# Causal attention with experts on one core: score products cut from four passes to two and three, operands split into a leading and a trailing part

## The chip, the cores and the metric

The kernel runs on one core of a Trainium2 chip. The metric is the device time of one execution in microseconds (us). Three executions of the kernel before took 3232.03, 3232.71 and 3240.1 us; the median is 3232.71 us.

## The reference

The input is x of 32 sequences, 512 tokens and 256 channels, in float32. Sixteen heads of 16 channels attend causally, twice:

```
q, k = x @ W_attn + b_attn          # queries and keys
y    = softmax(mask(q k^T / 4)) x   # first attention: the values are x itself
e    = x[1:] - y[:-1]               # what the first attention missed
k2   = x[:-1] @ W_k2 + b_k2
y2   = softmax(mask(q[1:] k2^T / 4)) e   # second attention, same queries
x    = layernorm(x + proj(y) + proj(y2))
x    = layernorm(x + experts(x))    # experts' output on one block of 512 tokens, in the first sequence
```

The softmax is taken with its true row maximum subtracted, so every score is needed twice: once for the maximum, once for the exponential. The results are float32.

## The kernel before

**Tiling.** A "group" is four heads of one sequence: 4 groups per sequence, 128 in all. The four heads of a group lie in the four quadrants of 32 partitions (rows) of SBUF; a head has 16 channels, so 16 rows of a quadrant are spare. The tiles `q_t` (5 buffers) and `kk_t` (6 buffers, with the keys of both attentions as index a = 0 and a = 1) hold one group each. A matmul between two quadrants uses 32 rows of TensorE, so four heads can stream side by side.

**Steps and slots.** `step(n)` runs for each group number n. It has five slots. In a slot, `slot(n, u)` issues on TensorE, interleaved by hand, two kinds of products: `maxima` for group n (scores with queries down the partitions, so VectorE can reduce the row maximum, L240) and `scores` for groups n-2 and n-3 (scores with keys down the partitions, of which ScalarE takes the exponential, L290, and GpSimd zeroes what lies above the diagonal, L294). In each slot each head has 512 columns of either kind. The heads are handled as two pairs; a slot takes four of PSUM's buffers `ps`, which are all four that there are. Between the slots other TensorE work stands in the lists `rest[0]` to `rest[4]`: `project` (L170), `augment` (transposes of the maxima, L248), `values` (products of the probabilities and the values, L335), `normalize` (transposes back, L350), `turn` and `attended` (output projection, L404 and L416). TensorE's order is exactly this one; the other engines' orders are set by a scheduler.

**The maximum.** It is written into a spare row of the quadrant through `augment`, added to the queries by GpSimd into `qm` (L253), and the keys carry a -1 in that row (from `b_qkk2`, put in by L133 and L136). One product then yields score minus maximum.

**The projection and its copies.** `project(two, m)` makes the queries (m = 0), the keys (m = 1) or the second keys (m = 2) of two groups at once, 2 x `two` and 2 x `two` + 1, with the heads packed densely. ScalarE adds the bias into `pk` (L174). One DMA for each head, on SP's queue, then carries 16 rows of 2 KB into the head's quadrant (L185): 8 DMAs for each m. In step n, `two` is n // 2 + 1. Before, m = 0 is projected in slot 1 of an even step, m = 1 and m = 2 in slots 1 and 2 of the odd step after it; the first group of the two is used from slot 0 of the next even step on.

**Experts.** Steps 10 to 17 also run one expert each (`hidden`, `down`, `load_expert`).

All products of `maxima` and `scores` are float32. The trace has two matmul records for each of them (L221: 12288 records, L275: 8192).

Of the kernel before, what the change touches and what calls it, by code (L numbers as in the profile page):

```python
# [9 lines left out]
F32 = mybir.dt.float32  # L10
BF16 = mybir.dt.bfloat16
# [11 lines left out]
NEG = -3.0e38  # L23
ALPHA = 1.702
LIMIT = 7.0


@with_exitstack
def block_kernel(
# [45 lines left out]
    bq_sb = const.tile([P, 3, NG], F32, name="bq_sb")  # L75
    nc.sync.dma_start(bq_sb, b_qkk2)
# [9 lines left out]
    q_t = [const.tile([P, T], F32, name=f"q_t{i}") for i in range(5)]  # L86
# [3 lines left out]
    bp_sb = const.tile([P, C], F32, name="bp_sb")  # L90
    nc.scalar.dma_start(bp_sb, b_proj.broadcast_to([P, C]))
    bp2 = const.tile([P, C], F32, name="bp2")
    nc.vector.tensor_add(bp2, bp_sb, bp_sb)
# [29 lines left out]
    v_pad = const.tile([P, NB, NG * GH, HS], F32, name="v_pad")  # L123
    e_pad = const.tile([P, NB, NG * GH, HS], F32, name="e_pad")
# [6 lines left out]
    zero = mx[0].rearrange("p n h s -> p (n h s)")  # L131
    for t in q_t:
        nc.scalar.activation(t, zero, AF.Identity, bias=bq_sb[:, 0, 0:1])  # L133
    for t in kk_t:
        for m in range(2):
            nc.scalar.activation(t[:, m], zero, AF.Identity, bias=bq_sb[:, 1 + m, 0:1])  # L136
# [5 lines left out]
    def load(b):  # L142
        s = seqs[b] = {}
        s["xT"] = seq.tile([P, NC, T], F32, tag="xT", name=f"xT{b}")
        nc.sync.dma_start(s["xT"], xT[b].rearrange("(c p) t -> p c t", p=P))
        s["x"] = seq.tile([P, NB, C], F32, tag="x", name=f"x{b}")
        nc.sync.dma_start(s["x"], x[b].rearrange("(n p) c -> p n c", p=P))
# [9 lines left out]
    def prepare(n):  # L157
        b, g = divmod(n, NG)
        s = seqs[b]
        heads = slice(g * GH, (g + 1) * GH)  # L160
        nc.gpsimd.tensor_copy(
            v_pad[:, :, heads, 0:HD], s["x"].rearrange("p n (h d) -> p n h d", d=HD)[:, :, heads]
        )


    def project(two, m):
        b, half = divmod(two, NG // 2)
        ps = bank2(f"pj{two}_{m}")
        for c in range(NC):
            nc.tensor.matmul(  # L170
                ps[:, 0], wq_sb[:, m, c, half * P : (half + 1) * P], seqs[b]["xT"][:, c], start=(c == 0), stop=(c == NC - 1)
            )
        pk = work.tile([P, T], F32, tag=f"half{(two * 3 + m) % 2}", name=f"pk{two}_{m}", bufs=1)
        nc.scalar.activation(pk, ps[:, 0], AF.Identity, bias=bp_qk[:, m, half : half + 1])  # L174
        for k in range(2):
            n = 2 * two + k
            d = groups.setdefault(n, {})
            if m == 0:
                t = d["q"] = q_t[n % len(q_t)]
            else:  # L180
                d["kk"] = kk_t[n % len(kk_t)]
                t = d["kk"][:, m - 1]
            for h in range(GH):
                r = (GH * k + h) * HD
                nc.sync.dma_start(t[HS * h : HS * h + HD], pk[r : r + HD])  # L185
# [12 lines left out]
    def maxima(n, u, pair):  # L198

        d = groups[n]  # L200
        parts, first, step, kinds = units[u]
        ps = bank2(f"sm{n}_{u}_{pair}")
        blocks = ps.rearrange("p h (k c) -> p h k c", c=P)
        work = []


        def mask(c, hh, rows):
            nc.tensor.matmul(  # L208
                blocks[:, hh, first::step, HS * c :],
                pick[rows, c],  # L210
                hide[rows, c, kinds[0] : kinds[1], HS * c :],
                start=(c == 0),
                stop=False,
            )

        for c in (0, *range(NB - 1, 0, -1)):
            work.append(((kinds[1] - kinds[0]) * (P - HS * c), partial(mask, c)))
        views = []

        def score(view, i, a, na, keys, stop, hh, rows):  # L220
            nc.tensor.matmul(  # L221
                view[:, hh, :, keys],
                d["q"][rows, i * P : (i + 1) * P],
                d["kk"][rows, a : a + na, keys],
                start=False,
                stop=stop,
            )

        for i, a, na, at in parts:
            nk = (i + 1) * P  # L230
            view = ps[:, :, at * P : at * P + na * nk].rearrange("p h (a k) -> p h a k", k=nk)
            views.append((view, mx[n % 2][:, i, NH2 * pair : NH2 * (pair + 1), HD + a : HD + a + na]))
            order = [slice(i * P, nk), slice(0, i * P)] if i else [slice(0, P)]
            for keys in order:
                stop = at == parts[-1][3] and keys == order[-1]
                work.append((4 * na * (keys.stop - keys.start), partial(score, view, i, a, na, keys, stop)))

        def largest():
            for view, to in views:
                nc.vector.tensor_reduce(to, view, AX.X, ALU.max)  # L240

        return work, largest

    def augment(n):
        d = groups[n]
        ps = bank2(f"mt{n}")
        for i in range(NB):
            nc.tensor.transpose(  # L248
                ps[:, 0, i * P : (i + 1) * P], mx[n % 2][:, i].rearrange("p h s -> p (h s)"), ident
            )  # L250
        d["qm"] = grp.tile([P, T], F32, tag="qm", name=f"qm{n}")
        nc.scalar.copy(d["qm"], ps[:, 0])  # L252
        nc.gpsimd.tensor_add(d["qm"], d["qm"], d["q"])  # L253
# [12 lines left out]
    def scores(n, u, pair):  # L266
        parts = [p for p in banks[u] if 0 <= n - p[0] < n_all]
        if not parts:
            return [], lambda: None
        ps = bank2(f"sc{n}_{u}_{pair}")  # L270
        pt = work.tile([P, NH2, T], F32, tag=f"pt{u}", name=f"pt{n}_{u}_{pair}")
        todo = []

        def score(d, a, j, at, hh, rows):
            nc.tensor.matmul(  # L275
                ps[:, hh, at * P : at * P + T - j * P],
                d["kk"][rows, a, j * P : (j + 1) * P],
                d["qm"][rows, j * P :],
                start=True,
                stop=True,  # L280
            )

        for a, j, at in parts:
            groups[n - a]["pt", a, j, pair] = pt[:, :, at * P : at * P + T - j * P]
            todo.append((4 * (T - j * P), partial(score, groups[n - a], a, j, at)))

        def exponentials():
            lo = parts[0][2] * P
            hi = parts[-1][2] * P + T - parts[-1][1] * P
            nc.scalar.activation(pt[:, :, lo:hi], ps[:, :, lo:hi], AF.Exp, scale=HD**-0.5)  # L290

            for a, j, at in parts:
                diag = pt[:, :, at * P : (at + 1) * P]
                nc.gpsimd.affine_select(  # L294
                    diag, diag, pattern=[[0, NH2], [1, P]], compare_op=ALU.is_ge, fill=0.0, base=-a,
                    channel_multiplier=-1,
                )

        return todo, exponentials
# [27 lines left out]
    def values(n, a):  # L327
# [5 lines left out]
        for j in order:  # L333
            for h in range(GH):
                nc.tensor.matmul(  # L335
                    ps[HS * h : HS * (h + 1), 0, j * P :],
                    vals[:, j, g * GH + h, :],
# [7 lines left out]
    def normalize(n, a):  # L345
# [20 lines left out]
        if a == 0:  # L366
# [3 lines left out]
            nc.gpsimd.tensor_sub(e_pad[:, :, g * GH : (g + 1) * GH, 0:HD], heads(s["xs"]), heads(s["y"]))  # L370
        else:
            y2 = work.tile([P, NB, GH * HD], F32, tag="y2", name=f"y2_{n}")
# [21 lines left out]
    def turn(b):  # L394
        s = seqs[b]

        s["xr"] = seq.tile([P, NB, C], F32, tag="xr", name=f"xr{b}", bufs=1)
        nc.sync.dma_start(s["xr"], x[b].rearrange("(n p) c -> p n c", p=P))
        nc.gpsimd.tensor_add(s["xr"], s["xr"], bp2.unsqueeze(1).to_broadcast([P, NB, C]))
# [7 lines left out]
    def attended(b, half):  # L407
# [6 lines left out]
        for i in range(2):  # L414
# [9 lines left out]
            s["h"][:, two], ps[:, 0].rearrange("p (i c) -> p i c", c=C), s["xr"][:, two]  # L424
# [59 lines left out]
    def load_expert(e):  # L484
        gu = moe["gu", e] = seq.tile([P, NC, 2, NF * P], F32, tag="gu", name=f"gu{e}")
# [3 lines left out]
        bd = moe["b_dn", e] = seq.tile([1, C], F32, tag="bd", name=f"bd{e}")  # L489
        nc.sync.dma_start(bd, b_dn[:, e])  # L490

    def hidden(e, f):
# [13 lines left out]
        for k in range(2):  # L506
            t = work.tile([P, T], F32, tag=f"half{k}", name=f"hf{e}_{f}_{k}", bufs=1)
            nc.vector.tensor_scalar(t, ps[:, k], moe["b_gu"][:, e, k, f : f + 1], LIMIT, ALU.add, ALU.min)  # L508
            half.append(t)
# [32 lines left out]
    def step(n):  # L542
# [3 lines left out]
        if r == 1 and b + 1 < B:  # L546
# [5 lines left out]
        if ready(n - 1):  # L552
            rest[3].append(lambda: augment(n - 1))
        if ready(n - 3):
            rest[1].append(lambda: normalize(n - 3, 0))
            rest[3].append(lambda: values(n - 3, 1))
            rest[4].append(lambda: normalize(n - 3, 1))
        two = n // 2 + 1
        if ready(2 * two):
            for m, s in [(0, 1)] if n % 2 == 0 else [(1, 1), (2, 2)]:  # L560
# [7 lines left out]
        if r2 == NG - 1 and 0 <= b2 < B:  # L568
            rest[0].append(lambda: attended(b2, 0))
            rest[2].append(lambda: attended(b2, 1))  # L570
# [98 lines left out]
```

## Time and profile before

| what | value |
|---|---|
| profiled execution: time, span | 3235.08 us, 3233.4 us |
| median of three executions | 3232.71 us |
| mean granted TensorE clock | 0.987 |
| PE (TensorE matmul) busy | 3057.4 us, 95% |
| PEld (weight load) busy | 1947.3 us, 60% |
| DVE (VectorE) busy | 1867.3 us, 58% |
| ACT (ScalarE) busy | 1734.0 us, 54% |
| POOL (GpSimd) busy | 1538.0 us, 48% |
| DMA | 148.12 MB, SP's queue 16.0% of the 16 DMA engines |

Busy time is the union of an engine's records. Matmuls on different quadrants overlap, so sums of matmul durations are larger than the time that they take. L12 is line 12 of the program text; `SPq` is SP's sequencer, which issues DMAs and is not counted as busy.

### The profile page before, as it was taken

The page shows a single profiled execution, that of the slowest core. Times are in us where ns is not written, and L with a number is a line of the kernel's source. Part 1 is how long each engine was busy: PE and PEld are TensorE (multiplying, and loading weights), DVE is VectorE, ACT ScalarE, POOL GpSimd, SP SyncE. Part 2 cuts the span into 40 slices and gives each one's busy share as a digit, 9 for nine tenths or more (in the row PEclk, how much of TensorE's full clock was granted, in tenths as well). Part 3 has the DMA queues.
Part 4 walks back from the last instruction along what each step waited for, and adds up shares of the span by engine and source line. Part 5 has one row for each costly group of instructions (what it writes and reads, how often), then busy time and mean ns, then how long its engine had stood idle before and what let it go on. Part 6 is the DMA issues. An engine that isn't in the chain of part 4 may idle for free.

```text
span 3233.4 us, 97999 instructions
## 1 busy us (share of the span) xinstructions
PE 3057.4 (95%) x42312; PEld 1947.3 (60%) x42312; DVE 1867.3 (58%) x2864; ACT 1734.0 (54%) x1956; POOL 1538.0 (48%) x2975
## 2 busy tenths in 40 slices
PE   5998889899999999999999999999999999999997
PEld 3665545566666666666666666666666666666664
DVE  4664444566666656566665666666556666665662
ACT  2554444455555555555555555555555555555554
POOL 4443434354554445454544455454445555544555
PEclk9999989999999999999999999999999999999998
DMA  4111111111111111111111111111111111111100
GB/s 113 32 32 49 41 39 37 39 52 46 46 41 54 38 54 48 53 45 38 50 41 51 51 50 51 41 41 54 38 54 48 53 45 44 45 47 44 39 26 21
DMA packets 144240, 148.12 MB, mean 46 GB/s; under 512 B 40984, under 2 KB 108992, under 8 KB 143808
## 3 DMA queue, kind: packets, MB, share of 16 engines
q1 hardware_dynamic: 143296, 141.42, 16.0%
q8 instruction: 333, 5.46, 0.7%
q14 instruction: 99, 0.81, 0.1%
q10 hardware_dynamic: 416, 0.39, 0.0%
q0 software_dynamic: 96, 0.04, 0.0%
HBM read 74.63 MB, written 16.78 MB: 28 GB/s over the span
## 4 chain that ended last, share of the span: by engine, by line
PE 61%; ACT 7%; POOL 7%; DVE 4%; issue 3%; SPq 0%; ACTq 0%; POOLq 0%; DMA 0%; DVEq 0%
PE sm L221 13%; PE av L335 13%; PE sc L275 12%; PE pj L170 10%; ACT pt L290 7%; PE po L416 4%; PE yt L350 3%; PE sm L208 3%; POOL h L445 2%; POOL pt L294 2%; PE mt L248 2%; DVE st L438 1%; DVE h L423 1%; POOL qm L253 1%; DVE mx L240 1%
## 5 line engine op out<-in xcount | busy, mean ns | idle before, releaser
L240 DVE TENSOR_REDUCE mx<-sm 128x2 f32<-128x1024 f32 (+3 forms) x1792 | 1541.1, 914 | 1092.1 <-PE sm L221 1083.0
L290 ACT ACTIVATE pt<-sc 128x1024 f32<-128x1024 f32 (+1 forms) x1282 | 1295.6, 1023 | 551.7 <-PE sc L275 529.4
L275 PE MATMUL sc<-qm,kk_t 32*128 32x256 f32 (+3 forms) x8192 | 1384.3, 448 | 26.2 <-ACT pt L290 7.8
L294 POOL TENSOR_SCALAR_AFFINE_SELECT pt<-pt 128x256 f32<-128x256 f32 x2048 | 797.3, 409 | 1268.5 <-ACT pt L290 1249.3
L221 PE MATMUL sm<-kk_t,q_t 32*128 32x128 f32 (+2 forms) x12288 | 1286.0, 351 | 12.8 <-DMA kk_t<-pk 12.8
L221 PEld LDWEIGHTS sm<-kk_t,q_t 32*128 32x128 f32 x12288 | 909.7, 187 | 29.3 <-DMA kk_t<-pk 13.6
L275 PEld LDWEIGHTS sc<-qm,kk_t 32*128 32x128 f32 x8192 | 711.1, 185 | 349.3 <-issue 206.9
L208 PE MATMUL sm<-hide,pick 32*128 32x128 bf16 (+5 forms) x10240 | 541.1, 216 | 8.5 <-DVE mx L240 7.8
L343 ACT COPY avs<-av 128x512 f32<-128x512 f32 x256 | 150.0, 586 | 533.8 <-PE av L335 533.8
L170 PE MATMUL pj<-xT,wq_sb 128*128 128x512 f32 x768 | 386.2, 627 | 29.5 <-DMA xT<-in_xT 19.5
L208 PEld LDWEIGHTS <-pick 32*128 32x128 bf16 x10240 | 351.4, 92 | 84.2 <-issue 67.4
L335 PE MATMUL av<-pt,v_pad 128*32 128x512 f32 (+3 forms) x4096 | 309.5, 437 | 41.6 <-POOL pt L294 40.7
L335 PE MATMUL av<-pt,e_pad 128*32 128x512 f32 (+3 forms) x4096 | 309.8, 443 | 10.8 <-DVE hf L508 3.6
L174 ACT ACTIVATE pk<-pj,bp_qk 128x512 f32<-128x512 f32 x192 | 131.9, 687 | 316.0 <-PE pj L170 219.6
L335 PEld LDWEIGHTS av<-pt,v_pad 128*32 128x32 f32 x4096 | 116.8, 109 | 223.1 <-issue 136.6
L170 PEld LDWEIGHTS pj<-xT,wq_sb 128*128 128x128 f32 x768 | 133.9, 194 | 167.9 <-issue 97.3
L335 PEld LDWEIGHTS av<-pt,e_pad 128*32 128x32 f32 x4096 | 124.3, 111 | 160.8 <-issue 126.3
L350 PE MATMUL yt<-ident,avs 128*128 128x128 f32 x1024 | 169.8, 289 | 21.1 <-ACT pt L290 20.3
L253 POOL TENSOR_TENSOR qm<-qm,q_t 128x512 f32<-128x512 f32 x128 | 163.9, 1281 | 16.9 <-ACT qm L252 9.6
L445 POOL TENSOR_SCALAR h<-h,mv,r 128x256 f32<-128x256 f32 x124 | 151.0, 1224 | 6.5
L350 PEld LDWEIGHTS yt<-ident,avs 128*128 128x128 f32 x1024 | 108.5, 142 | 65.9 <-ACT pt L290 50.5
L416 PE MATMUL po<-wp_sb,ysT 128*128 128x256 f32 x512 | 129.0, 396 | 5.3 <-ACT ysT L405 1.1
(78 smaller groups left out, 1442.8 us busy)
## 6 DMA issues: line engine op xcount, KB each, us to landing
kk_t<-pk SPq DMA_DIRECT2D x1024, 32.0 KB
xT<-in_xT SPq DMA_DIRECT2D x32, 512.0 KB
x<-in_x SPq DMA_DIRECT2D x32, 512.0 KB
q_t<-pk SPq DMA_DIRECT2D x512, 32.0 KB
xr<-in_x SPq DMA_DIRECT2D x32, 512.0 KB
out<-h SPq DMA_DIRECT2D x31, 512.0 KB
xs<-in_x SPq DMA_DIRECT2D x32, 384.0 KB
gu<-in_w_gu SPq DMA_DIRECT2D x8, 512.0 KB
```

Of the source, the lines that this page charges most:

```text
L170: nc.tensor.matmul(ps[:, 0], wq_sb[:, m, c, half * P : (half + 1) * P], seqs[b]["xT"][:, c], start=(c == 0), stop=(c == NC - 1))
L208: nc.tensor.matmul(blocks[:, hh, first::step, HS * c :], pick[rows, c], hide[rows, c, kinds[0] : kinds[1], HS * c :], start=(c == 0), stop ...
L221: nc.tensor.matmul(view[:, hh, :, keys], d["q"][rows, i * P : (i + 1) * P], d["kk"][rows, a : a + na, keys], start=False, stop=stop,)
L240: nc.vector.tensor_reduce(to, view, AX.X, ALU.max)
L253: nc.gpsimd.tensor_add(d["qm"], d["qm"], d["q"])
L275: nc.tensor.matmul(ps[:, hh, at * P : at * P + T - j * P], d["kk"][rows, a, j * P : (j + 1) * P], d["qm"][rows, j * P :], start=True, stop ...
L290: nc.scalar.activation(pt[:, :, lo:hi], ps[:, :, lo:hi], AF.Exp, scale=HD**-0.5)
L294: nc.gpsimd.affine_select(diag, diag, pattern=[[0, NH2], [1, P]], compare_op=ALU.is_ge, fill=0.0, base=-a, channel_multiplier=-1,)
L335: nc.tensor.matmul(ps[HS * h : HS * (h + 1), 0, j * P :], vals[:, j, g * GH + h, :], d["pt", a, j, h // NH2][:, h % NH2], start=(j == orde ...
L350: nc.tensor.transpose(ps[:, 0, i * P : (i + 1) * P], d["avs", a][:, i * P : (i + 1) * P], ident)
L416: nc.tensor.matmul(ps[:, 0, i * C : (i + 1) * C], s["ysT"][:, c, (2 * half + i) * P : (2 * half + i + 1) * P], wp_sb[:, c], start=(c == 0) ...
L445: nc.gpsimd.tensor_scalar(t[:, i], t[:, i], mv[:, k, 0:1], r[:, k : k + 1], ALU.subtract, ALU.mult)
```

## The change

The products become float32r products (a bit view of the same tiles, `half`), for which the operands are first split: `lead` is the projection written as float32r by ScalarE, `tail` is what is left of it, written by VectorE from the same PSUM bank.

- A key's quadrant holds the lead in its first 16 rows and the tail in its last 16 rows. The queries get two planes: plane 0 has the lead in both halves of the quadrant, plane 1 the tail in both. Plane 0 with the keys gives lead x (lead + tail), plane 1 gives tail x (lead + tail).
- `maxima` issues two such products where it had one float32 product, and the masks no longer open the bank.
- `scores` issues three: two with the planes and a third one, of the constants `minus` with the transposed maxima `m`, which subtracts the maximum. `qm` and its addition go; in their place two small GpSimd operations split the maxima.
- The copies into the quadrants are 32 DMAs for m = 0 (four per head) and 16 for m = 1 and for m = 2 (two per head).
- Work moves: m = 2 is projected in slot 2 of the even step, m = 1 in slot 1 and m = 0 in slot 2 of the odd step; `augment` and both `normalize` go to slot 0, both halves of `attended` to slot 1. The separate load of x for the output (`xr`) goes, `x` has 3 buffers, `v_pad` and `e_pad` are packed at 17 columns per head, experts' `gu` and `bd` have one buffer.

```diff
-        pk = work.tile([P, T], F32, tag=f"half{(two * 3 + m) % 2}", name=f"pk{two}_{m}", bufs=1)
-        nc.scalar.activation(pk, ps[:, 0], AF.Identity, bias=bp_qk[:, m, half : half + 1])
+        bias = bp_qk[:, m, half_ : half_ + 1]
+        lead = work.tile([P, T], F32, tag="half0", name=f"lead{two}_{m}")
+        nc.scalar.activation(half(lead), ps[:, 0], AF.Identity, bias=bias)
+        tail = work.tile([P, T], F32, tag="half1", name=f"tail{two}_{m}")
+        nc.vector.scalar_tensor_tensor(half(tail), ps[:, 0], bias, lead, ALU.add, ALU.subtract)
...
-                nc.sync.dma_start(t[HS * h : HS * h + HD], pk[r : r + HD])
+                first, second = slice(HS * h, HS * h + HD), slice(HS * h + HD, HS * (h + 1))
+                if m == 0:
+                    for rows in (first, second):
+                        nc.sync.dma_start(d["q"][rows, 0], lead[r : r + HD])
+                        nc.sync.dma_start(d["q"][rows, 1], tail[r : r + HD])
+                else:
+                    nc.sync.dma_start(d["kk"][first, m - 1], lead[r : r + HD])
+                    nc.sync.dma_start(d["kk"][second, m - 1], tail[r : r + HD])
...
         def score(view, i, a, na, k, start, stop, hh, rows):
             nc.tensor.matmul(
-                view[:, hh, :, keys],
-                d["q"][rows, i * P : (i + 1) * P],
-                d["kk"][rows, a : a + na, keys],
-                start=False,
+                view[:, hh],
+                half(d["q"][rows, k, i * P : (i + 1) * P]),
+                half(d["kk"][rows, a : a + na, : (i + 1) * P]),
+                start=start,
                 stop=stop,
             )
...
+        nc.gpsimd.tensor_copy(half(t[:, :, :, 0:2]), top)
+        nc.gpsimd.tensor_sub(half(t[:, :, :, 2:4]), top, t[:, :, :, 0:2])
...
-        nc.scalar.copy(d["qm"], ps[:, 0])
-        nc.gpsimd.tensor_add(d["qm"], d["qm"], d["q"])
+        nc.scalar.copy(half(d["m"]), ps[:, 0])
...
-        def score(d, a, j, at, hh, rows):
+        def score(d, a, j, at, k, hh, rows):
+            keys = minus[a][rows] if k == 2 else d["kk"][rows, a, j * P : (j + 1) * P]
+            queries = d["m"][rows] if k == 2 else d["q"][rows, k]
...
-            todo.append((4 * (T - j * P), partial(score, groups[n - a], a, j, at)))
+            for k in range(3):
+                todo.append((T - j * P, partial(score, groups[n - a], a, j, at, k)))
...
         if ready(n - 1):
-            rest[3].append(lambda: augment(n - 1))
+            rest[0].append(lambda: augment(n - 1))
         if ready(n - 3):
-            rest[1].append(lambda: normalize(n - 3, 0))
+            rest[0].append(lambda: normalize(n - 3, 0))
             rest[3].append(lambda: values(n - 3, 1))
-            rest[4].append(lambda: normalize(n - 3, 1))
+        if ready(n - 4):
+            rest[0].append(lambda: normalize(n - 4, 1))
         two = n // 2 + 1
         if ready(2 * two):
-            for m, s in [(0, 1)] if n % 2 == 0 else [(1, 1), (2, 2)]:
+            for m, s in [(2, 2)] if n % 2 == 0 else [(1, 1), (0, 2)]:
                 rest[s].append(lambda m=m: project(two, m))
...
-            rest[0].append(lambda: attended(b2, 0))
-            rest[2].append(lambda: attended(b2, 1))
+            for h in range(2):
+                rest[1].append(lambda h=h: attended(b2, h))
```

## The prediction

> **What bounds the kernel now.** First the page: busy time, the chain that ended last, the costliest groups, the DMA issues.
>
> ```profile
> PE 3057.4 (95%) x42312; PEld 1947.3 (60%) x42312; DVE 1867.3 (58%) x2864; ACT 1734.0 (54%) x1956; POOL 1538.0 (48%) x2975
> ...
> PE 61%; ACT 7%; POOL 7%; DVE 4%; issue 3%; SPq 0%; ACTq 0%; POOLq 0%; DMA 0%; DVEq 0%
> ...
> L275 PE MATMUL sc<-qm,kk_t 32*128 32x256 f32 (+3 forms) x8192 | 1384.3, 448 | 26.2 <-ACT pt L290 7.8
> ...
> L221 PE MATMUL sm<-kk_t,q_t 32*128 32x128 f32 (+2 forms) x12288 | 1286.0, 351 | 12.8 <-DMA kk_t<-pk 12.8
> ...
> kk_t<-pk SPq DMA_DIRECT2D x1024, 32.0 KB
> ```
>
> TensorE never rests, and the chain runs through it. SP and DMA have 0% of the chain: the copies into the quadrants (1024 for keys, 512 for queries, L185) are free now. Is TensorE saturated in the steady part too? The table by stretches for four steps (columns: length, busy us of PE, PEld, DVE, ACT, POOL, clock, DMA share, GB/s):
>
> ```profile
> 1535.00:1628.00 93.00, 90.53 (x1312) 58.56 (x1310) 56.40 (x87) 52.05 (x60) 45.84 (x89) 1.00 0.17 47
> ```
>
> Yes: 90.5 of 93 us at full clock, the others under 61%. The L248 transposes of groups 40 and 120 start at 1162.15 and 3024.83 us in the timeline, so a pair of steps (even, odd) takes 1862.68 / 40 = **46.57 us**. The timeline of TensorE prices one slot and its neighbours:
>
> ```profile
> 1583.74 0.49 PE L275 MATMUL sc<-qm,kk_t 32*128 32x384 f32 x2
> ...
> 1584.07 0.48 PE L275 MATMUL sc<-qm,kk_t 32*128 32x384 f32 x2
> ...
> 1584.39 0.27 PE L275 MATMUL sc<-qm,kk_t 32*128 32x128 f32 x2
> ...
> 1584.87 0.66 PE L350 MATMUL yt<-ident,avs 128*128 128x128 f32 x4
> ```
>
> A float32 product is two records; the 384-column records start 0.325 us apart, two passes each: 0.42 ns per column and pass. In the same timeline this slot runs from 1582.53 to 1584.87 (2.34 us). The five slots of that step sum to 12.3, mean 2.46; transposes take 0.6, a projection 1.89, values 2.29, both output halves 3.84, `turn` 0.97 (mean distances to the next start).
>
> Then SP's timeline, the timeline of the kernel's start (the one place where TensorE waits for a copy), and the table by stretches for the same start:
>
> ```profile
> 1573.02 11.14 SPq L185 DMA_DIRECT2D kk_t<-pk  x16
> ```
>
> ```profile
> 38.76 9.48 SPq L185 DMA_DIRECT2D kk_t<-pk  x14
> ...
> 40.70 4.00 PE L221 MATMUL sm<-kk_t,q_t 32*128 32x128 f32 x16 [12.75 <-DMA kk_t<-pk]
> ```
>
> ```profile
> 36.00:39.00 3.00, 0.00 (x0) 0.00 (x0) 0.00 (x0) 0.00 (x0) 0.00 (x0) 0.50 0.13 34
> 39.00:42.00 3.00, 1.30 (x5) 1.04 (x5) 0.00 (x0) 0.69 (x1) 0.00 (x0) 0.50 0.23 51
> 42.00:45.00 3.00, 3.00 (x35) 2.44 (x38) 0.60 (x1) 0.00 (x0) 0.00 (x0) 0.50 0.21 47
> 45.00:48.00 3.00, 3.00 (x30) 1.78 (x23) 3.00 (x5) 0.00 (x0) 0.00 (x0) 0.91 0.26 59
> ```
>
> SP issues one copy at a time, each for 0.58 us; bursts of 16 average **0.674 us** per copy over the trace. From an issue (38.76) to the product that waited for it (40.70) are 1.94 us. After 12.75 us of rest the clock is half (0.50), and stays so for almost 5 us of work.
>
> **What the Trainium skill says.** "FP8 and Floating Point Precision", TensorE Precision Notes: true float32 is four passes, a reduced-precision read of float32 fits the array's own width. The trace agrees on four (two records of two); no float32r product is in it. "TensorE: Matmul & The Clock Gate", Part 1: an idle window of about 3.4 us halves the clock until a busy window has passed; the table above agrees. Its Part 3: products on different row groups run side by side; the trace agrees for float32 (the x2 rows). "Trainium Kernel Development and Optimization", Key Constraints: the issuing engine's sequencer pays each DMA's issue time; SP's 0.58 us shows it.
>
> **The change part by part.**
>
> Products. Per slot and head: 4 x (512 + 512) columns become 3 x 512 + 2 x 512, that is 1536 fewer x 0.42 ns = 0.64 us. A slot goes from 2.46 to 1.82. Unknown is float32r's pass: at one pass 1.82, at two passes 1.82 + 2560 x 0.42 ns = 2.9; weights load once per product instead of twice and stay behind the streams. I take one pass. Ten slots a pair: 6.4 us saved on TensorE, 40.2 us left.
>
> Copies. L185 goes from 24 to 64 DMAs per pair of groups (32 + 16 + 16): 1536 become 4096. At 0.674 they hold SP for 43.1 us of each pair, against 16.2 before, and their order is what counts. In the odd step SP gets the 16 of m = 1, then the 16 queries of the first group, then those of the second. The even step's slot 0 needs the first 32. Before, m = 0 was a step earlier and 16 copies (8 + 8) stood there with time to spare. The new chain, from one release of slot 0 in an even step to the next:
>
> - the even step on TensorE: 5 x 1.82 + 0.6 + 1.3 + 1.89 + 2 x 2.29 + 1.92 (output halves every second time) = 19.4;
> - the odd step to the end of m = 1: 2 x 1.82 + 0.6 + 1.3 + 1.89 = 7.4;
> - `lead` on ScalarE 0.69 (row of L174) + 0.1; `tail` on VectorE 0.7 (nearest row: L423, 692 ns from PSUM) hides behind the first two copies;
> - 31 issues x 0.674 = 20.9, and 1.94 from the last issue to the product.
>
> Sum **50.4 us**. TensorE's rest of the odd step (3 x 1.82 + 1.89 + 4.58 + 0.5 = 12.4) fits into the 23.6 us of the last two items, so it stands idle for 11.2 us, its queue held at the first product of `maxima`, with everything behind it. SP itself is free in time: 16 left-over queries and m = 2's 16 end by about 25 us after the release, m = 1 is ready at 27.6. The six loads and stores that remain per sequence (xT, x, out, three for xs) stand in between, some 3 us per two pairs, in the gap.
>
> What the idle time adds: half clock for nearly 5 us, of which about 2.0 us are lost (0 if it doesn't drop, 3 at most). `values` (a = 0) now follows slot 4 directly, without the transposes between, and GpSimd's split of the maxima stands ahead of pair 0's last two selects (409 ns each, L294) and waits for VectorE's four reductions (914 ns mean): about 1.6 us late (0 to 2). Slots 1 and 2 of even steps follow each other on four PSUM buffers: 0.4 (0 to 1). The odd step's copies of these are under the stall. Pair: 54.4, rounded to **54.0**.
>
> Off the path: GpSimd loses 128 x 1.28 us (L253) and gets 256 small operations; ScalarE's work stays; VectorE gets 192 x 0.7 us = 134 us, 62% busy at most; the xr loads (32 issues) go. If any cover fails, the DVE share says how little: 2.1 us a pair.
>
> Sum. Of 63 pairs with a projection in them, 4 hold the experts, whose TensorE work in the odd step covers the stall: taken as unchanged (-26 to +30). 59 x (54.0 - 46.57) = +438. At the start 24 more copies stand ahead of the first products: 24 x 0.674, +16 to 27, taken 20. From the profiled execution's 3235.1 (span 3233.4), which is 2.4 above the median: 3235.1 + 458 - 2.4, about **3690 us**.
>
> **Rivals.**
>
> 1. SP's queue is no chain, only a load. If the copies were early enough, SP would set the floor: 4096 x 0.674 = 2761, some 115 for its other 227 issues, 45 at both ends: 2920 us, faster. For it: SP has 43 us of 46.6. Against it: the copies can't start before m = 1 is projected, one slot into the step before their use. The balance tips where the link of 0.8 + 31 issues + 1.94 is under 46.57 - 26.8 = 19.8 us: 0.55 us an issue. The fastest issue in the trace is 507 ns, the median 582.
> 2. float32r costs more than one pass, or its row groups don't stream side by side. Two passes: 7 slots in the chain x 1.08 = +7.5 a pair: 3690 + 59 x 7.5 = 4130 us. For it: no such product is in the trace.
> 3. The stall eats exactly the gain, 3233 us: pair 46.6, the same tipping point.
>
> **How the numbers follow.** The main case has 0.87: 3690, from 3460 (pair 50.4, nothing added, a little less at the start) to 3880 (pair 57: every addition at its upper bound and slots of 1.95). Rival 2 has 0.06, rival 1 0.05, rival 3 0.02. The range 3460 to 3880 leaves out the rivals, 0.13. 0.3% (10 us) is about what a measurement of this kernel can tell from no change: faster 0.05, same 0.02, slower 0.93.
>
> **What would show it.** Right: L185 (now 206 to 210) with 4096 issues at about 0.67 us; the group of `maxima` products with hundreds of us of idle time ended by the DMA of q_t, some 10 us at a time, every second step; PE near 75% busy; half clock after each stall; a pair of 54 us. Wrong: no such wait (rival 1), or slots of 2.5 us and more (rival 2).

## The result, and the profile after

The changed kernel takes **3789.1 us** (median of four executions, 3785.2 to 3795.3) where the kernel before takes 3232.4 beside it: ratio 1.172, 95% interval 1.169 to 1.174. It is slower, within the range that was given (3460 to 3880) and 99 us above the forecast of 3690. The profiled execution took 3795.26 us, its span is 3793.6.

From the page: busy times, the chain that ended last, the costliest groups, the DMA issues.

```profile
PE 3023.0 (80%) x41288; PEld 1901.7 (50%) x41288; DVE 2028.9 (53%) x3058; ACT 1711.0 (45%) x1939; POOL 1438.5 (38%) x3121
...
PE 39%; DVE 16%; SPq 15%; ACT 4%; DMA 3%; issue 3%; POOL 2%; POOLq 0%; DVEq 0%; ACTq 0%
...
L243 PE MATMUL sm<-kk_t,q_t 32*128 32x512 f32 (+2 forms) x7168 | 1339.5, 408 | 431.8 <-DMA q_t<-lead 272.7
...
q_t<-lead SPq DMA_DIRECT2D x1024, 32.0 KB
```

TensorE fell from 95% to 80% busy; SP's queue, 0% of the chain before, holds 15% of it. The products of `maxima` (L221 before, L243 now) had 12.8 us of idle time ahead of them and have 431.8, most of it ended by the DMA of `q_t`. The last line stands for four alike (`lead` and `tail` into `q_t` and `kk_t`): 4096 copies, as counted. The table by stretches for four steps (before: 90.53 us of PE in 93, clock 1.00) has nearly the same busy time of TensorE in a longer stretch and at a lower clock:

```profile
1805.00:1916.00 111.00, 90.33 (x1286) 57.58 (x1287) 62.39 (x93) 52.44 (x60) 42.80 (x93) 0.92 0.23 59
```

A pair of steps, measured as before between the first transposes (now L277) of groups 40 and 120, takes **55.38 us** against 46.57. The timeline of TensorE and that of SP show the stall. First TensorE:

```profile
1821.73 0.34 PE L303 MATMUL sc<-q_t,kk_t 32*128 32x384 f32 x2
...
1821.91 0.34 PE L303 MATMUL sc<-m,minus 32*128 32x384 f32 x2
...
1832.41 1.99 PE L188 MATMUL pj<-xT,wq_sb 128*128 128x512 f32 x4
...
1856.89 0.76 PE L243 MATMUL sm<-kk_t,q_t 32*128 32x512 f32 x1 [1.83 <-DMA q_t<-lead]
1858.44 1.11 PE L277 MATMUL mt<-ident,mx 128*128 128x128 f32 x4
```

Then SP:

```profile
1835.14 1.14 SPq L209 DMA_DIRECT2D kk_t<-lead  x2
...
1846.00 0.53 SPq L206 DMA_DIRECT2D q_t<-lead  x1
...
1855.43 0.59 SPq L207 DMA_DIRECT2D q_t<-tail  x1
```

The two 384-column records start 0.18 us apart, 0.47 ns per column with the starts' rounding, where each of the two records of a float32 product had 0.325: a float32r product is one pass. The products of `maxima` were also merged: 6144 float32 products (12288 records) before, 3584 in each of the two planes now, for the same columns. The projection of m = 1 ends at 1834.40; SP issues 16 copies of keys and then the first group's 16 of queries, the last at 1855.43; the product that waited starts at 1856.89. Slot 0 of an even step, from the end of `values` to the first transposes, takes 9.40 us on average, that of an odd step 2.33: the copies delay TensorE by **7.06 us per pair**. The delay comes in pieces, as the copies of one head after another land, and not as one wait of some 10 us.

The table by stretches, with the clock as the third number from the end of each line, shows the half clock (0.50) that a stall leaves behind:

```profile
1850.00:1855.00 5.00, 2.31 (x31) 1.32 (x27) 1.23 (x1) 1.61 (x2) 1.13 (x3) 0.85 0.22 52
1855.00:1860.00 5.00, 3.17 (x30) 2.74 (x30) 1.23 (x1) 1.41 (x2) 0.35 (x2) 0.50 0.20 46
```

The waits of TensorE, summed over the trace (us, times, longest), have one more surprise:

```profile
PE sm L243 <- DMA q_t<-lead: 272.7, 169, 8.1
PE av L364 <- POOL pt L323: 82.5, 132, 5.0
PE av L364 <- DVE top L266: 80.8, 132, 0.7
PE sm L243 <- DVE tail L195: 61.6, 149, 0.5
```

Below the first line stand short waits, mostly of 0.4 to 0.7 us, for VectorE and GpSimd, several in each step. A pair had 1.2 us of idle time on TensorE before; now it has 10.3, of which 4.6 are for copies and nearly all of the other 5.7 are these. (The rest of the 7.06 us of delay is slot 0's products themselves, a few at a time and partly at half clock.)

### The profile page after: what moved, and what is told of

Read it like the earlier page. It is cut to its first block, busy times and chain, and to the rows that moved or that the text cites. A ratio compares the mean times of both kernels' runs of the same rounds, so it can differ in the third digit from the quotient of the medians.

```text
span 3793.6 us, 100200 instructions
## 1 busy us (share of the span) xinstructions
PE 3023.0 (80%) x41288; PEld 1901.7 (50%) x41288; DVE 2028.9 (53%) x3058; ACT 1711.0 (45%) x1939; POOL 1438.5 (38%) x3121
## 4 chain that ended last, share of the span: by engine, by line
PE 39%; DVE 16%; SPq 15%; ACT 4%; DMA 3%; issue 3%; POOL 2%; POOLq 0%; DVEq 0%; ACTq 0%
DVE top L266 10%; PE av L364 8%; PE pj L188 8%; PE sc L303 7%; SPq L207 6%; SPq L206 6%; PE sm L243 5%; PE po L443 3%; PE yt L379 3%; DMA q_t<-lead 3%; PE sm L234 2%; PE mt L277 2%; DVE tail L195 2%; ACT lead L193 2%; ACT pt L319 2%
## 5 line engine op out<-in xcount | busy, mean ns | idle before, releaser
L266 DVE TENSOR_REDUCE top<-sm 128x2 f32<-128x1024 f32 (+3 forms) x1792 | 1560.4, 914 | 1132.8 <-PE sm L243 574.2
L243 PE MATMUL sm<-kk_t,q_t 32*128 32x512 f32 (+2 forms) x7168 | 1339.5, 408 | 431.8 <-DMA q_t<-lead 272.7
L303 PE MATMUL sc<-q_t,kk_t 32*128 32x256 f32 (+3 forms) x8192 | 1183.6, 360 | 38.0 <-DVE y L402 19.5
L243 PEld LDWEIGHTS sm<-kk_t,q_t 32*128 32x128 f32 x7168 | 675.3, 196 | 603.6 <-issue 267.0
L303 PEld LDWEIGHTS sc<-q_t,kk_t 32*128 32x128 f32 x8192 | 695.8, 195 | 325.6 <-issue 199.8
L303 PE MATMUL sc<-m,minus 32*128 32x256 f32 (+3 forms) x4096 | 687.3, 332 | 0.0
L303 PEld LDWEIGHTS sc<-m,minus 32*128 32x128 f32 x4096 | 414.6, 198 | 11.0
L234 PEld LDWEIGHTS <-pick 32*128 32x128 bf16 x10240 | 333.2, 97 | 10.3 <-issue 1.1
L195 DVE SCALAR_TENSOR_TENSOR tail<-pj,bp_qk,lead 128x512 fp32r<-128x512 f32 x192 | 144.1, 751 | 312.8 <-ACT lead L193 304.8
L193 ACT ACTIVATE lead<-pj,bp_qk 128x512 fp32r<-128x512 f32 x192 | 132.0, 687 | 264.8 <-PE pj L188 206.1
L379 PEld LDWEIGHTS yt<-ident,avs 128*128 128x128 f32 x1024 | 160.1, 178 | 4.2 <-ACT pt L319 2.1
```

The lines of the kernel that those rows point to most:

```text
L195: nc.vector.scalar_tensor_tensor(half(tail), ps[:, 0], bias, lead, ALU.add, ALU.subtract)
L234: nc.tensor.matmul(blocks[:, hh, first::step, HS * c :], pick[rows, c], hide[rows, c, kinds[0] : kinds[1], HS * c :], start=False, stop=False,
L243: nc.tensor.matmul(view[:, hh], half(d["q"][rows, k, i * P : (i + 1) * P]), half(d["kk"][rows, a : a + na, : (i + 1) * P]), start=start, s ...
L303: nc.tensor.matmul(ps[:, hh, at * P : at * P + T - j * P], half(keys), half(queries[:, j * P :]), start=(k == 0), stop=(k == 2),)
L379: nc.tensor.transpose(ps[:, 0, i * P : (i + 1) * P], d["avs", a][:, i * P : (i + 1) * P], ident)
```

## The experiments

**Theory:** the pair is as long as a chain: the even step on TensorE, the odd step to the end of m = 1, `lead`, 31 issues in SP's queue, the landing. ("TensorE's part of the chain" below is its first two pieces together: from the start of the last product in slot 0 of an even step that waited for a copy to the end of the next m = 1.) **Rivals:** the products themselves lose the time; SP's queue is a load only; or the DMA engines, not the issues, are the limit. All ratios below are against the kernel before on the same chip, with 95% intervals.

### The copies alone

The kernel before, its float32 products, the projections placed as in the change, and as many copies as the change has:

```diff
                 nc.sync.dma_start(t[HS * h : HS * h + HD], pk[r : r + HD])
+                for _ in range(1 if m else 3):
+                    i = unused["i"] = (unused["i"] + 1) % 8
+                    nc.sync.dma_start(spare[HD * i : HD * (i + 1)], pk[r : r + HD, 0 : T - 32])
...
-            for m, s in [(0, 1)] if n % 2 == 0 else [(1, 1), (2, 2)]:
+            for m, s in [(2, 2)] if n % 2 == 0 else [(1, 1), (0, 2)]:
```

> The kernel before with nothing of the change but its copies: the projections stand as in the changed kernel (m = 2 in slot 2 of the even step, m = 1 and m = 0 in slots 1 and 2 of the odd step), and each head's copy on SP's queue is followed by 3 unused ones (m = 0) or 1 (m = 1, 2) into a spare tile, 64 per pair. Products stay float32. Theory (the chain through SP sets the pair): even step 22.3 + odd step to the end of m = 1 7.9 + 0.8 + 28 x 0.674 + 1.94 = 51.8, and about 2 of half clock: pair 53.8, about 3680 us. Rival (the float32r products or the moved transposes cost the time, the copies are hidden): about 3233 us.

4092.3 us, ratio 1.265 (1.262 to 1.268): slower than either foresaw. The waits of GpSimd name the reason:

```profile
POOL xr L405 <- DMA xr<-in_x: 252.9, 30, 61.9
```

The load of `xr` stands behind the copies in SP's queue, GpSimd waits for it with the selects behind, and `values` on TensorE waits for those (4.2 us per pair). The change itself had dropped this load. So the experiment was repeated with the load on another queue (`nc.scalar.dma_start(s["xr"], ...)`):

> The kernel before with its float32 products, the projections placed as in the changed kernel, 40 more copies per pair into a tile that nothing reads, and the xr load on ScalarE's queue, so that GpSimd no longer waits for it behind the copies. Chain: even step with slots of 2.46 22.6 us, odd step to the end of m = 1 8.7, lead 0.8, 31 x 0.674 = 20.9, landing 1.9: pair 54.9 us, about 3740 us. If the extra copies hurt only by the xr load (the second victim in b1), about 3233 us; if the queue is no chain but a mere load of 43 us, also about 3233.

3836.2 us, ratio 1.185 (1.183 to 1.187). The pair is 54.5 us, with TensorE waiting for the copies:

```profile
PE sm L227 <- DMA q_t<-pk: 227.1, 162, 8.6
```

The copies alone, with no float32r product, cost about what the whole change costs (1.185 against 1.172). That the pair lies so near the expected 54.9 is in part luck. With the unused copies behind each real one, the last copy that slot 0 needs is mostly the 29th, so 28 issues stand in the link and not 31: 18.9 us at 0.674, measured 19.2. TensorE's part of the chain made up for over half of that, with 32.4 us instead of 31.3, at a mean clock of 0.93; the expectation had left out the half clock. The time is 96 us over the expectation, from outside the steady part: the 16 steps around the experts take 675 us where the kernel before takes 550.

### The products alone

The changed kernel, with 24 of the 64 copies per pair:

```diff
-                    for rows in (first, second):
-                        nc.sync.dma_start(d["q"][rows, 0], lead[r : r + HD])
-                        nc.sync.dma_start(d["q"][rows, 1], tail[r : r + HD])
+                    nc.sync.dma_start(d["q"][first, 0], lead[r : r + HD])
...
-                    nc.sync.dma_start(d["kk"][second, m - 1], tail[r : r + HD])
```

> The changed kernel with only 24 of the 64 copies per pair (lead of the queries into the first rows of plane 0, lead of the keys into the first rows); the other rows and the second plane are zeroed once, so the tails and the doubled lead are left out of the products, which keep their number and shapes. If the stall is the chain of copies alone: the 7.06 us of stall and some 2 us of half clock go, pair 46.3 us, about 3230 us, no better than the kernel before, since new waits of 4.4 us take what the products save. If the products' saving had come through in full (slots 1.82, no new waits), 40.5 to 41, about 2900 us. If the products or the new engine work are themselves dearer than thought: above 3400 us.

3246.1 us, ratio 1.003 (1.002 to 1.005); pair 46.73. The stall and the half clock are gone, and yet nothing is won. TensorE's busy time per pair is 40.78 us against 45.37 before, 4.6 us less; its idle time is 5.95 against 1.19, 4.8 us more. Its waits:

```profile
PE av L363 <- DVE top L265: 82.7, 134, 0.7
PE av L363 <- POOL pt L322: 82.4, 132, 5.0
PE mt L276 <- DVE top L265: 74.2, 125, 1.0
```

So the change has two costs of different kinds: a chain of copies, and short waits that take all that the products save. The run also shows that the new places of the projections make no stall by themselves. What 64 copies would cost with the queries' projection at its old place, a step earlier, was not run.

### Fewer issues, or an earlier first group

Two planes in one DMA (`lead` and `tail` in one tile `both`), 16 copies per pair fewer, eight of them ahead of the stall:

```diff
-                        nc.sync.dma_start(d["q"][rows, 0], lead[r : r + HD])
-                        nc.sync.dma_start(d["q"][rows, 1], tail[r : r + HD])
+                        nc.sync.dma_start(d["q"][rows], both[r : r + HD])
```

> The changed kernel, with lead and tail in one tile, so that one copy carries both planes of the queries: m = 0 has 16 copies instead of 32, the same bytes; 24 issues instead of 32 stand between m = 1 and slot 0 of the even step. Theory (chain): the stall of 7.06 us a pair loses 8 x 0.68 = 5.4, what is left is too short for half clock, 2 more: pair 48.0 instead of 55.4, about 3350 us. Rival A (SP's load as such, 43 us a pair): 11 us less of it, so a gain too, of a size that it doesn't give. Rival B (bytes moved, or the products): 3789 us, no change.

3493.4 us, ratio 1.078 (1.076 to 1.081). Slot 0 of an even step takes 5.05 us instead of 9.40: 4.35 less, for 8 issues fewer in the link (8 x 0.674 = 5.4). The bytes are the same as in the changed kernel; only the issues are fewer. The pair is 50.7 where 48.0 was expected. The issues of the link did fall, from 20.94 to 15.86 us, but a copy of two planes lands later: 2.58 us pass from the last issue to the product that waited, against 1.62 in the changed kernel. And TensorE's part of the chain became only 0.5 us shorter, where 2 us of half clock were expected to go.

The same number of DMAs, but m = 1's copies of the second group wait until the first group's queries are issued. SP's order is written out for it, the experts' loads go to GpSimd's queue, and at the start the queries are projected last:

```diff
+        carry(0)
+        if m == 1:
+            later.append(partial(carry, 1))
+        else:
+            while later:
+                later.pop()()
+            carry(1)
```

> The changed kernel with SP's queue in the order of the program, in which the 8 copies of m = 1 for the second group come behind the queries of the first group. 64 copies as before; the experts' loads go to GpSimd's queue, since SP would deadlock on them. Theory (chain): 24 issues in the link instead of 32, the same gain as with two planes per copy: about 3350 us. Rival A (SP's load): 3789 us, since SP has as much to do as before. Rival B: 3789 us.

3861.3 us, ratio 1.193 (1.191 to 1.195): a miss. The link did what was expected, slot 0 fell to 4.49 us. But another wait took its place:

```profile
PE pj L190 <- DMA xT<-in_xT: 312.8, 30, 19.5
```

In program order the next sequence's `xT` load stands behind the queries' copies, and the projection of m = 2 needs it. Both edits together:

> Two planes per copy and the first group first: 16 issues in the link. Theory (chain): 0.8 + 15 x 0.68 + 1.94 = 13 us, under the 15 or so of TensorE's work in the rest of the odd step, so no stall at all: pair 46.3, about 3255 us, which is then what the products themselves are worth against the kernel before (nothing). If the products' saving of 6.4 us a pair were there once the stall is gone: pair 42, about 3000 us.

3445.2 us, ratio 1.064 (1.063 to 1.066), pair 49.8 where 46.3 was expected. There is no stall at slot 0 (2.30 us), but the wait for `xT` is left, 2.07 us per pair. Moving that load forward:

```diff
-        if r == 2 and b + 1 < B:
+        if r == 1 and b + 1 < B:
             load(b + 1)
```

> As a3 (two planes per copy, first group first), but the loads of the next sequence's x and its transpose are issued one step earlier, at the start of the odd step before, ahead of the query copies. If the wait for xT in a3 (2.07 us per pair of steps) came only from that load's place in SP's queue, it is gone and no stall takes its place: pair 49.8 - 2.1 - 0.3 (clock) = 47.4 us, about 3310 us. If SP is simply full (its load, not the order), the wait moves elsewhere and the pair stays near 49.8, 3440 us.

3275.1 us, ratio 1.012 (1.011 to 1.014), pair 46.73: the same pair as with the products alone, now with all the data carried. The first cost is gone by fewer issues and their order (with the experts' loads on another queue).

### Another queue for half of the copies

The changed kernel, the tails' copies on `nc.gpsimd` instead of `nc.sync`:

> The changed kernel with all 64 copies, the 32 of the tails issued from GpSimd's queue. If the stall is SP's queue of issues, only 15 issues x 0.674 = 10.1 us of link are left in SP's queue, under the 15.2 us that the odd step has: no stall from q_t<-lead, pair 46.7 to 48, 3280 to 3350 us, unless GpSimd's own issues (each at SP's 0.6 us: 19 us a pair, in front of selects and splits) make values late; then up to 55. If the DMA engines or the writes into the quadrants were the limit, moving the issue would change nothing: 3790 us.

3657.2 us, ratio 1.130 (1.126 to 1.135), pair 53.0. The stall at slot 0 is gone (2.50 us), so SP's queue was the limit and not the DMA engines. In its place stands the rival cost that the expectation named; the timeline of GpSimd, and TensorE's wait for it:

```profile
1808.24 3.96 POOL L210 DMA_DIRECT2D kk_t<-tail  x8
1812.20 1.47 POOL L323 TENSOR_SCALAR_AFFINE_SELECT pt<-pt 128x256 f32<-128x256 f32 x4
```

```profile
PE av L364 <- POOL pt L323: 337.3, 111, 8.7
```

Eight issues hold GpSimd for 3.96 us, and the selects that `values` needs stand behind them. The Trainium skill, "Trainium Kernel Development and Optimization", Key Constraints, says that issuing from several engines "only saves the sequencer's issue time". Here that time was the cost, and it was paid on the other engine instead.

### The short waits

The order of the steps of the kernel before (`augment` in `rest[3]`, `normalize` in `rest[1]` and `rest[4]`, `attended` in `rest[0]` and `rest[2]`), and the split of the maxima on VectorE, on top of the version with the earlier load:

> As a4, and the steps stand again where the kernel before had them (transposes of the maxima after slot 3, of the two value sums after slots 1 and 4, the output halves after slots 0 and 2), and the split of the maxima runs on VectorE instead of GpSimd. The copies are as in a4. If the some 4.4 us of short waits per pair (values on GpSimd and VectorE 2.4, scores on y 0.6, projection on VectorE 0.5, products on tail 0.9) come from this order and this engine, about 3.5 of them go: pair 44.0 us, about 3100 us, under the kernel before. If they come with the products themselves (new PSUM pace), the pair stays at 47.4 and the time at 3310 us.

3197.3 us, ratio 0.988 (0.987 to 0.990), pair 45.5: 1.25 us off, of the 3.4 expected. The waits on GpSimd went; others came for them (the transposes of `normalize` now wait 1.2 us per pair for VectorE). Then the split alone, with the order of the change:

```diff
-        nc.gpsimd.tensor_copy(half(t[:, :, :, 0:2]), top)
-        nc.gpsimd.tensor_sub(half(t[:, :, :, 2:4]), top, t[:, :, :, 0:2])
+        nc.vector.tensor_copy(half(t[:, :, :, 0:2]), top)
+        nc.vector.tensor_sub(half(t[:, :, :, 2:4]), top, t[:, :, :, 0:2])
```

> As a4, with one edit: the two small operations that split the maxima (0.46 us together on GpSimd) run on VectorE, the order of the steps stays. If they are what makes values (a = 0) wait for GpSimd's selects (1.16 us per pair in a4), that wait goes, and pair 46.7 falls to 45.6, about 3205 us, as a5 did with the order as well. If the wait is that of the selects themselves behind the exponentials, which a slot of 2.0 us no longer covers, it stays and the pair stays at 46.7, 3275 us; a5's gain is then that of its order.

**3173.4 us**, ratio 0.982 (0.980 to 0.985), pair 45.1: 1.8% faster than the kernel before, and better than with the old order. The wait that it takes away is this one, with the earlier load and the split on GpSimd:

```profile
PE av L374 <- POOL pt L333: 83.2, 132, 5.0
```

With the split on VectorE that line is gone from the top of the waits, which now begin with

```profile
PE av L374 <- DVE top L276: 77.5, 126, 0.7
```

The timeline of GpSimd in the changed kernel shows why two operations of 0.46 us together cost 0.8 us a step:

```profile
1822.91 0.77 POOL L323 TENSOR_SCALAR_AFFINE_SELECT pt<-pt 128x256 f32<-128x256 f32 x2 [3.21 <-ACT pt L319]
1824.27 0.21 POOL L273 CAST mx<-top 128x32 fp32r<-128x32 f32 x1 [0.59 <-DVE top L266]
...
1824.77 0.77 POOL L323 TENSOR_SCALAR_AFFINE_SELECT pt<-pt 128x256 f32<-128x256 f32 x2
```

GpSimd sits 0.59 us at the split, until VectorE has reduced the last maxima, with the next selects queued behind it.

### Is it the chain? Two trials with the stall in place

If the chain sets the pair, an edit counts only by what it takes out of the chain. The same split on VectorE, in the changed kernel with all its copies:

> The changed kernel with a6's edit alone: the split of the maxima on VectorE, all 64 copies as they are. In a4, without a stall, this edit was worth 1.65 us per pair, 0.8 of it in the even step. If the pair is set by the chain through SP's queue, only what lies in the chain counts: the even step's 0.8 us come through, and what the odd step gains only lengthens the stall: pair 55.4 - 0.8 = 54.6, about 3745 us. If waits add up along TensorE whatever the copies do, all of it comes: pair 53.7, about 3690 us.

3736.8 us, ratio 1.156 (1.154 to 1.158), pair 54.41: 0.97 less than the changed kernel, where the same edit without the stall gave 1.65. From the transposes of the even step to those of the odd one the time fell by 0.96 us (24.81 to 23.85); slot 0 of the even step grew from 9.40 to 10.17. The odd step's gain went into the stall, as the chain says.

And TensorE kept at work through the stall:

```diff
+            if s == 0 and n % 2 == 0 and 2 <= n < n_all:
+                for k in range(4):
+                    ps = bank2(f"keep{n}_{k}")
+                    for i in range(6):
+                        nc.tensor.matmul(ps[:, 0].rearrange("p (c k) -> p c k", k=P), pick[:, 0], pick, start=(i == 0), stop=(i == 5))
             slot(n, s)
```

> The changed kernel with 24 products of 128x512 bf16 (0.215 us each, 5.2 us in all) ahead of slot 0 of every even step, in four tiles of the PSUM rotation that nothing reads: TensorE works through most of the stall. If the stall only shifts work by its own length, nothing changes: the chain doesn't run through TensorE's idle time, pair 55.4, 3790 us. If the half clock behind the stall lengthens the even step, which is in the chain (products alone took 23.2 us from the transposes of an even step to those of the odd step, the changed kernel 24.75, and slot 0's last products and the transposes themselves some 0.5 more), about 2.0 us per pair go: 53.4, about 3670 us, with the clock at 1.0 in the even steps. If the extra products lie behind the copies and come out late: above 3800 us.

3753.1 us, ratio 1.161 (1.159 to 1.163), pair 54.28: 1.10 less, by doing 5.35 us more work. (The added products start 0.216 us apart for 512 columns, 0.42 ns per column, which is the forecast's price of one pass.) The table by stretches behind the added products, in such a stall (clock third from the end), shows no drop:

```profile
1847.00:1852.00 5.00, 3.45 (x55) 2.16 (x53) 1.22 (x1) 1.02 (x1) 0.76 (x2) 1.00 0.23 53
```

The half clock is real. TensorE's part of the chain fell from 32.07 to 30.82 us, 1.25 less, of which the 31 issues of SP took back 0.25 (21.19 us); 2.0 had been forecast. Over the trace the mean clock is 0.968 instead of 0.909, so a little of the half clock is left.

## Why the prediction was right, point by point

| term, us | predicted | measured |
|---|---|---|
| SP per copy, start to start | 0.674 | 0.676 |
| TensorE's part of the chain: release of slot 0 to the end of the next m = 1 | 26.8, with its additions 30.8 | 32.07 |
| 31 issues of the link | 20.9 | 20.94 |
| end of m = 1 to the first copy | 0.8 | 0.75 |
| last issue to the product that waited | 1.94 | 1.62 |
| columns per pass, float32r | one pass | one pass |
| a slot with 384 and 128 columns | 2.34 less 0.64 | 1.92, without waits |
| TensorE's busy time per pair | 6.4 less | 4.6 less (products alone) |
| stall per pair | 11.2, all idle | 7.06 of delay, 4.6 of it idle |
| half clock per pair | 2.0 (0 to 3) | 1.1 (1.25 in TensorE's part) |
| `values` (a = 0) late, in the even step | 1.6 (0 to 2) | 0.58 for GpSimd, 0.61 for VectorE |
| pair | 54.0 | 55.38 |
| first product of `maxima` later | 20 | 20.4 |

**The mechanism was right.** The bound is the chain through SP's queue between m = 1 and slot 0, and copies alone reproduce it. Its four measured parts, averaged over the 40 pairs, make up the whole pair: 32.07 + 0.75 + 20.94 + 1.62 = 55.38. TensorE is 80% busy, where 75% was forecast. `tail` at 751 ns (0.7 was taken) lies beside the first copies, as said. That the pair came out only 1.4 us longer than 54.0 (1.0 longer than the unrounded sum, 54.4) is in part luck: the half clock was taken 0.75 us too long in TensorE's part and the landing 0.3, and these hide half of the 2.0 us by which TensorE's part is longer for other reasons.

**What was mis-sized is the TensorE part of the chain.** The prediction let a slot fall to 1.82 us with nothing else waiting, but for `values` and 0.4 us of PSUM. The slot itself measured 1.92; why 0.42 and not 0.64 us are saved is not settled. The larger miss is the list of short waits. TensorE's idle time without the waits for copies was 1.2 us per pair and became 5.7: `values` for VectorE 1.22 and for GpSimd 1.16, `maxima` for `tail`, which holds its PSUM buffer, 1.04, the projection 0.66, the transposes of the maxima 0.59, `scores` behind the transposes of both attentions 0.34, and some of 0.2 and less. The prediction had priced `tail` as hidden behind the copies, and forgot that it is also the last reader of the projection's PSUM tile. The work that empties the PSUM buffers did not become shorter: VectorE's reductions take 2.56 us per slot on average in both kernels. In one slot they take 2.49 us and ScalarE's two exponentials 1.94:

```profile
1821.72 2.49 DVE L266 TENSOR_REDUCE top<-sm 128x2 f32<-128x768 f32 x4 [2.06 <-PE sc L303]
```

```profile
1821.82 1.94 ACT L319 ACTIVATE pt<-sc 128x1024 f32<-128x1024 f32 x2 [0.43 <-PE sc L303]
```

So a slot of 1.92 us is shorter than the work that empties its buffers, which one of 2.34 nearly covered. That the waits for VectorE come from this is argued from the lengths; no run shows it, and which of the buffers' readers decides each wait was not tried.

**Why the stall was smaller than 11.2 and the pair no shorter.** In the odd step the short waits and longer slots fill time in which TensorE would otherwise have stood before the copies. They cost nothing there; the trial of the split with the stall in place showed it. In the even step they lengthen the chain. The forecast's range held because its upper end, a pair of 57, took slots of 1.95 and every addition at its bound.

**The sum.** The first product of `maxima` starts 20.4 us later (40.70 before, 61.07 now), as taken (20). For the rest the transposes are no common mark: they stood after slot 3 of a step and stand after slot 0, 13 us earlier. The projection of m = 1 kept its place in the odd steps. Measured there, the first comes 31.6 us later, so 11.2 are lost in the first steps, which the prediction didn't have. The 53 pairs outside the experts' stretch take 472.6 more, 8.9 each where 7.43 was taken. The nine pairs around the experts take 48.1 more, of which the five without experts explain 45: the expert steps are about unchanged, as taken. From the last m = 1 to the end it is 7.9 more, a stretch in which the last stall lies; products alone, without a stall, take 2.3 less there. Together 560.2, the difference of the two spans.

**The rivals.** SP as a load only (2920 us) and the even balance (3233) would have needed a link under 19.8 us; it measured 0.75 + 20.94 + 1.62 = 23.3. The case with fewer issues shows the other side of the tipping point: with two planes per DMA and the first group first the stall is zero. Two passes per float32r product (4130 us) are excluded by the records.

## What to carry to other kernels

Count the DMAs that an engine must issue between the moment when their source is ready and their first use, at the measured time per issue, and not only the queue's total: 31 issues made a chain here, though SP had time to spare over the pair. Merge them, order them by first use, and look at what else stands behind them in the queue (`xr` and `xT` were the next to be late). When products get shorter, compare a stage's length with the time that the other engines take to empty its PSUM buffers: here 4.6 us of saved TensorE work per pair were met by 4.8 us of new waits, and two small operations on GpSimd, in line with its selects, cost 1.65 us of each pair.

## What was not expected of the hardware

- The clock halves without one long gap. In the stall at 1850 us TensorE had rested 1.43 us at most when the clock fell at 1853.5, and never more than 1.83 us before it was back at 1860.3; from 1850.1 on it had worked 44% of the time. The table by stretches of 1 us, clock third from the end:

```profile
1853.00:1854.00 1.00, 0.04 (x1) 0.00 (x0) 0.97 (x1) 0.83 (x1) 0.00 (x0) 0.76 0.19 47
1854.00:1855.00 1.00, 0.70 (x1) 0.28 (x1) 0.25 (x1) 0.20 (x1) 0.73 (x2) 0.50 0.26 57
```

  The Trainium skill, "TensorE: Matmul & The Clock Gate", Part 1, which the prediction used, puts the drop after an idle window of about 3.4 us; here a window of which 44% was work was enough.

- GpSimd issues these DMAs somewhat faster than SP: median 484 ns in the run with the tails there (3.96 us for eight in a row), against 587 on SP (676 from start to start).
- SP's time for an issue is not even. A copy takes 0.59 us mostly, but 158 of the 4096 take over 1.2 us (up to 2.0); the load of a single row, L173, which comes once for each sequence, holds the queue for 3.27 us in the median (2.69 to 6.53), longer than five copies.
- Products that nothing needs made the kernel 36 us faster (3753.1 against 3789.1), since they kept the clock mostly at 1.00 (mean 0.987 in the steady part, against 0.914).
